# A graph layer's edge scatter on one core: twelve more quads take the grouped way

## The chip, the cores and the metric

One core of a Trainium2 chip. The metric is device time in microseconds, the median of several runs. TensorE is called PE here, VectorE DVE, ScalarE ACT, GpSimd POOL and SyncE SP. SP's queue only issues DMAs, in the order of the program, and a DMA whose wait isn't fulfilled holds up those behind it.

## The reference

A graph layer on 6250 nodes of 128 features and 200,000 edges. `dst` is sorted, so the gather from `x[idx_j]` reads nearly neighbouring rows; `src`, the target of the sum, is random.

```
idx_i, idx_j = src, dst                       # 200000 each
h    = relu(layernorm(x))                     # 6250 x 128
x1   = h @ W_in
W_ij = (softplus(f_ij @ W_f1 + b_f1) - ln 2) @ W_f2 + b_f2     # f_ij: 200000 x 20
x_ij = x1[idx_j] * (W_ij * f_ij_cutoff)
out  = segment_sum(x_ij, idx_i, 6250)
return x + (softplus(out @ W_o1 + b_o1) - ln 2) @ W_o2 + b_o2
```

## The kernel before

The edges are cut into chunks of 128 and quads of four chunks, 391 quads. One item of the main loop brings in one quad; the stages of a quad lie in successive items (`s1_`, `s2_`, `s3_`), and each item emits its instructions in fixed points: `L` (loads), `D0`, `D1`, `PE0`, `A0`, `A1`, `AX`, `DM`, `DR`, `PE1`, `PE2`, `A2`, `D2`, `S` (scatters). The table `AT` gives each step of the side work an offset in items and a point; `put` and `at` enter it there. What stands in one point of one item runs in the order in which it was entered. Nothing is reordered later.

Every quad has the same product: PE makes `z` (L374), ACT its softplus `a` (L379, L384), PE gathers `xg` by one-hots (L559) and multiplies `W` (L556, L567), ACT scales `xg` into `xc` (L572), DVE multiplies both (L582). Then there are three ways to the sum over `src`:

- Plain quads (the first of the ungrouped, `s3_pe`, `s3_copy`): a 128 x 128 equality matrix `eq` and matmuls `pp` (L594) add up edges of the same node in a chunk, and POOL scatters each chunk's sums `s` with its indices `ji` into one of four accumulators in HBM by an adding indirect DMA (L644, `acc<-s,ji`).
- Listed quads (every other ungrouped quad, `LB` to `LE`): the products `s` (six buffers) are scattered directly (L644, `acc<-s,lji`), four scatters for a quad. Edges whose node occurs twice in a chunk go to separate list rows (`l_eq`, `l_count` (L437), and twelve windows of 16 quads), which are summed at the end of a window (`l_load` L513, `l_sum` L531) and scattered once more.
- Grouped quads (`mpq`, in which `mpi` is the quad's number): no scatter for each chunk. DVE splits the product `pt` into three bf16 parts (L746), makes a permutation one-hot `pm` (L732) from a ranking for eight quads (`rank_*`, L655 to L725), PE permutes (`permute`, tile `pq`, L758), ACT copies (`perm_out`, tile `sg`, L766), SP regroups into `mst` (`regroup`, L773). Edges that overflow their group are summed for two grouped quads together (`over_*`: `po` L781, `mo`, `orow` L804, `oeq` L812, `osum` L818 to L820) and scattered once (`acc<-os,oji`).

Eight grouped quads form a round. A round is summed in four unit rounds: `unit_oh` makes a one-hot `so` (L845) for each quad, nine buffers, `unit_pe` multiplies 96 matmuls `un` (L860) into all four PSUM banks of tag `B`, and `unit_evac` adds these into the SBUF accumulator `accT` (L871). `unit_slots` places the four unit rounds over the time of the next round, in items that bring in a grouped quad whose third predecessor is not grouped. In such an item `permute` of the quad four items back moves to the item ahead.

Near the end, accumulator 0 gets no more scatters after the one numbered `RET`; `r0_load` (L1171, tile `r0t`) then fetches it, three items after the one with that scatter at the earliest, and PE transposes it (`rtp`, L1178). When all scatters have landed, a tail of 13 tiles adds up accumulators 1 to 3 and `accT` and multiplies by the output weights (from L1513).

Before, quads 8, 10, 12, ... 388 are grouped (191), 188 are listed and 12 plain.

Of the kernel before, what the change touches and what calls it, by code (L numbers as in the profile page):

```python
# [8 lines left out]
BF16 = mybir.dt.bfloat16  # L9
I32 = mybir.dt.int32  # L10
# [10 lines left out]
P = 128  # L21
# [5 lines left out]
OVC = 128  # L27
SLOTS = GRP * BCAP + OVC
MP0 = 8
MPGAPS = (2,)  # L30
MPEND = 1
RND = 8
RKQ = 8
ULAG = 7
# [41 lines left out]
def tile_gnn(ctx: ExitStack, tc: tile.TileContext, x, fB, cT, srcT, srcr, srci, dstr, win_, wf1, wf2, bias, bo1c, wo1,  # L76
# [25 lines left out]
    mpq = sorted_quads(NQ)  # L102
    mpi = {q: n for n, q in enumerate(mpq)}
    rounds = unit_rounds(mpq)
    uslots = unit_slots(rounds)
    units = {i for us in uslots for i in us}
# [31 lines left out]
    wk = edge.enter_context(tc.tile_pool(name="wk", bufs=2))  # L138
# [669 lines left out]
        mp[q]["row"] = t  # L808

    def over_eq(q):  # L810
        eq = wk.tile([P, P], BF16, tag="oeq", name="oeq", bufs=1)
        nc.vector.tensor_scalar(eq, mp[q].pop("row")[:, :P], mp[q]["so"], None, op0=ALU.is_equal)  # L812
        mp[q]["eq"] = eq

# [104 lines left out]
    with tc.manual_schedule():  # L919
# [126 lines left out]
        def at(i, point, fn, *a):  # L1046
            hooks.setdefault((i, point), []).append((fn, a))

        def put(name, base, fn, *a, busy=()):
            d, point = AT[name]  # L1050
            i = max(clear(base + d, busy) if busy else base + d, 0)
            at(i, point, fn, *a)
            return i
# [66 lines left out]
        busy = units | {prep_start(g) + k for g in range(1, NG) for k in range(5)}  # L1120
# [85 lines left out]
        if spread:  # L1206
            k = clear(mid + 9, busy, 2)
# [3 lines left out]
            k = clear(NQ - 1, busy, 2)  # L1211
# [25 lines left out]
        for r in range(-(-len(mpq) // RKQ)):  # L1237
# [5 lines left out]
            k = put("rk_count", i, rank_count, r, busy=units)  # L1243
            k = max(k + 1, i + AT["rk_own"][0])
            at(k, AT["rk_own"][1], rank_own, r)
            k = clear(max(k, i + AT["rk_over"][0]), units)
            at(k, AT["rk_over"][1], rank_over, r)
            k = max(k + 1, i + AT["rk_slot"][0])
# [5 lines left out]
        for w in range(NW):  # L1254
            for g in range(wsize[w] // 4):
# [9 lines left out]
                k = put("l_dup", i, l_dup, w, g)  # L1265
# [12 lines left out]
            k = clear(i + AT["l_sum"][0], units)  # L1278
# [4 lines left out]
            k = put("l_int", k, over_int, ("L", w))  # L1283
# [4 lines left out]
        for q in mpq:  # L1288
            put("pm", q, perm_oh, q)
            put("rem1", q, part_rem, q, 1)  # L1290
            put("rem2", q, part_rem, q, 2)
            put("ext", q, part_ext, q)
            if q + 4 in units:
                for s in range(4):
                    at(q + 3, "PE2", permute, q, s)
                for s in range(4):
                    at(q + 3, "PE2", perm_out, q, s)
                for h in range(2):
                    at(q + 4, "L", regroup, q, h)
            else:  # L1300
                for s in range(4):
                    put(f"p{s}", q, permute, q, s)
                    put(f"o{s}", q, perm_out, q, s)
                for h in range(2):
                    put(f"rg{h}", q, regroup, q, h)
            if mpi[q] % 2 or q == mpq[-1]:
                k = mpq[mpi[q] + 1] if mpi[q] + 1 < len(mpq) else q + 2
                put("over_pe", k, over_pe, q)
                put("over_out", k, over_out, q)
                put("over_idx", q, over_idx, q)  # L1310
                put("over_dg", q, over_dg, q)
                k = put("over_row", q, over_row, q, busy=units)
                put("over_eq", k, over_eq, q)
                k = put("over_sum", q, over_sum, q, busy=units)
                put("over_copy", k, over_copy, q)
                put("over_ji", k, over_ji, q)
                k = put("over_int", k, over_int, q)
                at(k, "S", over_scatter, q)
        last = mpq[-1]
        for r, us in enumerate(uslots):  # L1320
            for s, k in enumerate(us):
                for h in range(3):
                    d, point = AT[f"so{h}"]
                    at(max(k + d, us[s - 1] if s else uslots[r - 1][3] if r else 0), point, unit_oh, r, s, h)
                put("unit", k, unit_pe, r, s)
                put("evac", k, unit_evac, r, s)

# [100 lines left out]
    with tc.For_i(0, redo, 1):  # L1428
# [8 lines left out]
        with tc.For_i(0, trips, 1) as ci:  # L1437
# [12 lines left out]
                cm, engines=[SP], min_val=0, max_val=EP // P - 1,  # L1450
                skip_runtime_bounds_check_because="a column of the table")
            nc.sync.dma_start(xcol, dropd[:, bass.ds(cr, 1)])
            sb = wk.tile([P, P], I32, bufs=1, tag="oeq", name="fsb")
            nc.sync.dma_start(sb, srcr.rearrange("s e -> (s e)")[bass.ds(ci * P, P)].unsqueeze(0).to_broadcast([P, P]))
            ft = wk.tile([P, P], BF16, tag="oh", name="fft")
            nc.vector.memset(ft[96:P, :], 1.0)
# [32 lines left out]
            eq = wk.tile([P, P], F32, tag="eq", name="feq", bufs=3)  # L1489
# [3 lines left out]
            s = wk.tile([P, P], F32, bufs=1, tag="dg", name="fs")  # L1493
# [118 lines left out]
def sorted_quads(nq):  # L1612
    qs, q = [], MP0
    while q < nq - MPEND:
        qs.append(q)
        q += MPGAPS[(len(qs) - 1) % len(MPGAPS)]
    return qs
# [10 lines left out]
def unit_slots(rounds):  # L1628
    end = rounds[-1][-1]
    grouped = {q for qs in rounds for q in qs}  # L1630
    out, used = [], set()
    for r, qs in enumerate(rounds):
        a = qs[-1] + ULAG
        last = r == len(rounds) - 1
        step = 2 if last else (rounds[r + 1][-1] - qs[-1]) / 4
        us = []
        for s in range(4):
            i = a + int(s * step)
            while i in used or (not last and i <= end and not UCLASSES[UCLASS](i, grouped)):
                i += 1  # L1640
            used.add(i)
            us.append(i)
        out.append(us)
    return out
# [10 lines left out]
def clear(i, busy, n=1):  # L1655
    while any(i + k in busy for k in range(n)):
        i += 1
    return i
# [11 lines left out]
def prep_start(g):  # L1670
    busy = unit_its(sorted_quads(4 * PREP_GAP * (g + 8)))
    return clear(7 + PREP_GAP * (g - 1), busy, 2) - 1
# [100 lines left out]
```

## Time and profile before

| | |
|---|---|
| median of 3 runs | 1912.47 us (1911.3 to 1914.54) |
| the profiled execution | 1918.46 us, span 1916.7 us |
| mean granted clock of PE | 0.96 |
| instructions | 55067 |
| scatters on POOL | 907 (751 listed, 48 plain, 108 of sums) |
| items 0 to 390 end (last softplus) | at 1821 us |
| output tail | from 1867 us |

How to read the lines below. A group's row names line, engine, operation, tiles, shapes and count, then busy time in us and the mean length of one in ns, then the engine's idle time ahead of it with what ended that time. A stretch's row gives start and end, length, and for each engine that has work busy time and number of instructions, then PE's granted clock, the share of the DMA engines' time and GB/s; without a filter the engines are PE, PE's weight load (PEld), DVE, ACT, POOL. A wait's row has who waited for what, us in total, how often, and the longest. "issue" is time for which the profile shows no cause.

### The profile page before, as it was taken

Reading aid. Unit: us, or ns where it says so; the run is one execution under the profiler, and the core shown is the slowest. Engines: PE = TensorE matmul, PEld = TensorE weight load, DVE = VectorE, ACT = ScalarE, POOL = GpSimd, SP = SyncE. Lnnn points to the kernel's source line nnn. Section 1 sums busy time; section 2 is a strip of 40 time slices with the busy share of each in tenths; the row PEclk is TensorE's granted clock in tenths of the full one; section 3 lists DMA queues with packets and bytes.
Section 4 is the critical chain, followed back from the end, with each engine's and each line's share of the span. In section 5 each row is a group of like instructions: output and inputs, shape, how many; then the busy total and the mean of one; then the engine's idle time right before and its main releaser. Section 6 shows DMA issues by size and latency. Waiting matters only on the chain. (4 is left out here: it accounts for less than half of the span.)

```text
span 1916.7 us, 55067 instructions
## 1 busy us (share of the span) xinstructions
PE 1676.3 (87%) x19124; PEld 1142.4 (60%) x19124; DVE 1600.0 (83%) x4692; ACT 1449.6 (76%) x4045; POOL 1509.3 (79%) x960
## 2 busy tenths in 40 slices
PE   4678898989998989989989989999999999978976
PEld 3555566656666666665656656666666566655644
DVE  5768897988898899899889888898897897976657
ACT  4668777867887888887878878887887888866615
POOL 5577768778888888888888888888888888887755
PEclk8789999999999999999999999999999999998988
DMA  8888888878888888888888888888888888868757
GB/s 294 229 197 198 191 186 173 175 153 160 172 180 168 162 177 172 162 188 162 164 175 180 168 171 178 174 179 174 173 183 155 172 183 170 169 121 185 130 116 267
DMA packets 366238, 339.58 MB, mean 177 GB/s; under 512 B 86685, under 2 KB 329292, under 8 KB 365956
## 3 DMA queue, kind: packets, MB, share of 16 engines
q1 hardware_dynamic: 233189, 269.78, 49.5%
q0 software_dynamic: 132208, 66.05, 33.0%
q8 instruction: 151, 2.47, 0.5%
q14 instruction: 132, 1.07, 0.2%
q10 hardware_dynamic: 558, 0.20, 0.0%
HBM read 151.16 MB, written 108.80 MB: 136 GB/s over the span
## 5 line engine op out<-in xcount | busy, mean ns | idle before, releaser
L644 POOL DMA_INDIRECT acc<-s,lji x751 | 1210.0, 1611 | 269.4 <-issue 177.0
L572 ACT ACTIVATE xc<-xg,cb 128x128 f32<-128x128 f32 x1564 | 447.5, 374 | 179.7 <-PE z L374 92.5
L567 PEld LDWEIGHTS W<-w,a 128*128 128x128 f32 x3128 | 430.0, 199 | 64.2 <-issue 50.9
L860 PE MATMUL un<-so,mst 32*128 32x392 bf16 x9168 | 425.1, 329 | 18.1 <-ACT sg L766 7.9
L567 PE MATMUL W<-w,a 128*128 128x128 f32 x3128 | 430.7, 282 | 0.8 <-issue 0.5
L766 ACT CAST sg<-pq 128x388 bf16<-128x388 f32 x764 | 342.1, 497 | 75.0 <-DMA mst<-sg 48.5
L758 PE MATMUL pq<-pt,pm 128*128 128x388 bf16 x1528 | 328.5, 337 | 30.5 <-ACT os L825 9.6
L860 PEld LDWEIGHTS <-mst 32*128 32x128 bf16 x9168 | 251.5, 94 | 166.8 <-issue 37.6
L384 ACT ACTIVATE a<-a,con 128x512 f32<-128x512 f32 x391 | 282.8, 723 | 11.6
L746 DVE TENSOR_TENSOR pt<-pt 128x512 f32<-128x512 f32 x382 | 259.6, 680 | 0.0
L871 DVE TENSOR_TENSOR accT<-un,accT 128x392 f32<-128x392 f32 x368 | 182.1, 556 | 80.0 <-PE z L374 26.6
L379 ACT ACTIVATE a<-z 128x512 f32<-128x512 f32 x391 | 243.7, 623 | 6.3 <-PE z L374 6.3
L758 PEld LDWEIGHTS <-pm 128*128 128x128 bf16 x1528 | 143.6, 98 | 145.4 <-issue 56.9
L845 DVE TENSOR_SCALAR so<-iot,mst 128x392 bf16<-128x392 f16 x764 | 215.6, 333 | 4.3 <-PE un L860 2.9
L374 PE MATMUL z<-ft,ws 123*128 123x512 bf16 x391 | 154.8, 397 | 63.9 <-DVE s L582 13.2
L582 DVE TENSOR_TENSOR s<-W,xc 128x512 f32<-128x512 f32 x188 | 128.8, 685 | 93.8 <-ACT xc L572 56.5
L644 POOL DMA_INDIRECT acc<-os,oji x108 | 173.6, 1607 | 40.9 <-issue 18.3
L732 DVE TENSOR_SCALAR pm<-iotp,pos 128x384 bf16<-128x384 f16 x764 | 201.3, 323 | 0.0
L582 DVE TENSOR_TENSOR pt<-W,xc 128x512 f32<-128x512 f32 x191 | 130.4, 683 | 49.2 <-ACT xc L572 23.9
L559 PE MATMUL xg<-wn,oh 63*128 63x128 bf16 x1564 | 158.0, 222 | 12.1 <-DVE oh L391 7.3
L556 PE MATMUL W<-b2rep,onesb 64*128 64x512 bf16 x391 | 155.1, 397 | 0.0
L781 PE MATMUL po<-pt,pm 128*128 128x387 bf16 x764 | 153.1, 343 | 1.3 <-DVE pt L746 1.1
(214 smaller groups left out, 1840.9 us busy)
## 6 DMA issues: line engine op xcount, KB each, us to landing
mst<-sg SPq DMA_DIRECT2D x764, 97.0 KB
sb<-src SPq DMA_DIRECT2D x100, 256.0 KB
rb<-reld SPq DMA_DIRECT2D x194, 128.0 KB
fsd<-f SPq DMA_DIRECT2D x49, 480.0 KB
ft<-fsd SPq DMA_DIRECT2D x96, 240.0 KB
fb<-in_fB_dram SPq DMA_DIRECT2D x49, 320.0 KB
ft<-fsd SPq DMA_DIRECT2D x96, 160.0 KB
acc<-s,lji POOLq DMA_INDIRECT x751
```

The lines of the kernel that those rows point to most:

```text
L379: nc.scalar.activation(a, st[q]["z"], AF.Exp)
L384: nc.scalar.activation(a, a, AF.Ln, bias=half, scale=0.5)
L567: nc.tensor.matmul(W[:, c, :], st[q]["a"][:, c * P:(c + 1) * P], w2, start=False, stop=(c == 3))
L572: nc.scalar.mul(xc[:, c, :], st[q]["xg"][:, c, :], late["c", q // CQ][:, 4 * (q % CQ) + c:4 * (q % CQ) + c + 1])
L582: nc.vector.tensor_tensor(m[:, :, :P], st[q]["W"], st[q]["xc"], op=ALU.mult)
L644: nc.gpsimd.indirect_dma_start(out=accs[k][:rows, :], out_offset=bass.IndirectOffsetOnAxis(ap=ji, axis=0), in_=s, in_offset=None, compute_ ...
L732: nc.vector.tensor_scalar(pm[:, c], iotp, rk[r]["pos"][:, 4 * j + c:4 * j + c + 1], None, op0=ALU.is_equal)
L746: nc.vector.tensor_tensor(pt[:, :, k * P:(k + 1) * P], a, high(a), op=ALU.subtract)
L758: nc.tensor.matmul(t[:, :MW], mp[q]["pm"][:, c, s * P:(s + 1) * P], high(mp[q]["pt"][:, c:c + 1, :MW])[:, 0], start=(c == 2 * h), stop=(c ...
L766: nc.scalar.copy(mp[q]["sg", h][:, s], mp[q].pop(("q", k))[:, :MW])
L845: nc.vector.tensor_scalar(so, iotw[:, :GN], w[:, 3 * P // 2:3 * P // 2 + 1], None, op0=ALU.is_equal)
L860: nc.tensor.matmul(ts[g][:, :GN], mp[q]["ms", s // 2][v, s % 2, k * P:(k + 1) * P], mp[q]["oh"][v], start=(q == qs[0] and k == 0), stop=(q ...
```

## The change

`sorted_quads` now steps 2, 2, 2, 2, 1, 2, 2, 2, so that 15 items hold eight grouped quads where 16 did, and in every eight there is one pair in adjacent items. 203 quads are grouped, 172 listed (eleven windows) and 16 plain. There are 26 rounds, the last of three quads, where there were 24, the last of seven. Of a quad whose successor is grouped too, the second half of the copies and the regroup move to points `PE1` and `PE2` four items on. `oeq` gets a second buffer, the overflow sum is kept at least one item behind the row it needs, and a one-hot that would come earlier than the unit round ahead of it is written at the end of that round's item.

```diff
-MPGAPS = (2,)
-MPEND = 1
+MPGAPS = (2,2,2,2,1,2,2,2)
+MPEND = 2
...
-        eq = wk.tile([P, P], BF16, tag="oeq", name="oeq", bufs=1)
+        eq = wk.tile([P, P], BF16, tag="oeq", name="oeq", bufs=2)
...
                 for s in range(4):
                     put(f"p{s}", q, permute, q, s)
-                    put(f"o{s}", q, perm_out, q, s)
+                    if q + 1 in mpi and s > 1:
+                        at(q + 4, "PE1", perm_out, q, s)
+                    else:
+                        put(f"o{s}", q, perm_out, q, s)
                 for h in range(2):
-                    put(f"rg{h}", q, regroup, q, h)
+                    if q + 1 in mpi and h:
+                        at(q + 4, "PE2", regroup, q, h)
+                    else:
+                        put(f"rg{h}", q, regroup, q, h)
...
-                k = mpq[mpi[q] + 1] if mpi[q] + 1 < len(mpq) else q + 2
+                k = mpq[mpi[q] + 1] if mpi[q] + 1 < len(mpq) else q + 3
...
-                k = put("over_sum", q, over_sum, q, busy=units)
+                k = put("over_sum", max(q, k + 1 - AT["over_sum"][0]), over_sum, q, busy=units)
...
-                    at(max(k + d, us[s - 1] if s else uslots[r - 1][3] if r else 0), point, unit_oh, r, s, h)
+                    b = us[s - 1] if s else uslots[r - 1][3] if r else 0
+                    at(max(k + d, b), "D2" if k + d <= b else point, unit_oh, r, s, h)
```

The unit rounds stood four items apart (90 of 95 distances). Now they follow at distances of 2, 5, 4 and 4 (29 of 103 are 2). On DVE, in the middle of the program, the add into `accT` (four instructions) that empties the banks of one unit round, and the ten rows behind it, before:

```order
L871 TENSOR_TENSOR accT<-un,accT 128x392 x4
L582 TENSOR_TENSOR pt<-W,xc 128x4x128
L324 TENSOR_REDUCE fmax<-fb 128x1
L732 TENSOR_SCALAR pm<-iotp,pos 128x384 x4
L525 TENSOR_SCALAR leq<-orow,idl 128x128
L444 TENSOR_SCALAR ldup<-lcnt,con 128x16
L391 TENSOR_SCALAR oh<-rb,con 128x512
L746 TENSOR_TENSOR pt<-pt 128x4x128
L582 TENSOR_TENSOR s<-W,xc 128x4x128
L746 TENSOR_TENSOR pt<-pt 128x4x128
L845 TENSOR_SCALAR so<-iot,mst 128x392 x3
```

and now, at a place where two unit rounds stand two items apart:

```order
L871 TENSOR_TENSOR accT<-un,accT 128x392 x4
L582 TENSOR_TENSOR pt<-W,xc 128x4x128
L845 TENSOR_SCALAR so<-iot,mst 128x392 x3
L732 TENSOR_SCALAR pm<-iotp,pos 128x384 x4
L444 TENSOR_SCALAR ldup<-lcnt,con 128x16
L746 TENSOR_TENSOR pt<-pt 128x4x128
L582 TENSOR_TENSOR s<-W,xc 128x4x128
L746 TENSOR_TENSOR pt<-pt 128x4x128
L391 TENSOR_SCALAR oh<-rb,con 128x512
L830 SCALAR_TENSOR_TENSOR ojd<-os,con,ojd 128x1
L871 TENSOR_TENSOR accT<-un,accT 128x392 x4
```

Before, the first one-hots `so` of the next unit round come ten rows after the add and the next add into `accT` stands another 14 rows on; now five of them stand above these rows, ahead of the first add, the last three right behind it, and the next add follows ten rows after the first.

On POOL, in the middle of the program, scatters of listed products (`s,lji`) and of overflow sums (`os,oji`; the numbers tell the four accumulators apart), before:

```order
L644 DMA acc_77<-os,oji 6400x128
L644 DMA acc_78<-s,lji 7296x128
L644 DMA acc_75<-s,lji 7296x128
L644 DMA acc_76<-s,lji 7296x128
L644 DMA acc_77<-s,lji 7296x128
L644 DMA acc_78<-s,lji 7296x128
L644 DMA acc_75<-s,lji 7296x128
L644 DMA acc_76<-s,lji 7296x128
L644 DMA acc_77<-s,lji 7296x128
L644 DMA acc_78<-os,oji 6400x128
L644 DMA acc_75<-s,lji 7296x128
```

and now:

```order
L644 DMA acc_77<-s,lji 7168x128
L644 DMA acc_78<-os,oji 6400x128
L644 DMA acc_75<-os,oji 6400x128
L644 DMA acc_76<-s,lji 7168x128
L644 DMA acc_77<-s,lji 7168x128
L644 DMA acc_78<-s,lji 7168x128
L644 DMA acc_75<-s,lji 7168x128
L644 DMA acc_76<-os,oji 6400x128
L644 DMA acc_77<-s,lji 7168x128
L644 DMA acc_78<-s,lji 7168x128
L644 DMA acc_75<-s,lji 7168x128
```

Between two sums there stood eight listed scatters; now two sums stand together, then four listed scatters, then the next sum. In all POOL issues 687 listed, 64 plain and 113 other scatters, 864 for 907.

More of the change, by code (lines that the diff above doesn't have):

```diff
@@ L1452, in tile_gnn @@
             nc.sync.dma_start(xcol, dropd[:, bass.ds(cr, 1)])
-            sb = wk.tile([P, P], I32, bufs=1, tag="oeq", name="fsb")
+            sb = wk.tile([P, P], I32, bufs=2, tag="oeq", name="fsb")
             nc.sync.dma_start(sb, srcr.rearrange("s e -> (s e)")[bass.ds(ci * P, P)].unsqueeze(0).to_broadcast([P, P]))
```

## The prediction, made before the run

> **What bounds the kernel now.** I read the engine shares first, then the stretches of the main loop, then who waits for whom inside it, then the SP queue near the end. The two busiest resources are TensorE and the scatters on POOL:
>
> ```profile
> PE 1676.3 (87%) x19124; PEld 1142.4 (60%) x19124; DVE 1600.0 (83%) x4692; ACT 1449.6 (76%) x4045; POOL 1509.3 (79%) x960
> ```
>
> The stretches (time, then busy time of each engine) show a steady loop:
>
> ```profile
> 200.00:400.00 200.00, 180.57 (x2087) 122.54 (x2077) 173.41 (x527) 157.87 (x448) 151.27 (x96) 0.98 0.83 176
> 400.00:600.00 200.00, 181.33 (x2115) 123.17 (x2115) 173.10 (x535) 156.46 (x443) 165.92 (x103) 0.96 0.81 165
> 1200.00:1400.00 200.00, 186.54 (x2289) 126.11 (x2288) 172.94 (x493) 166.13 (x464) 166.64 (x106) 1.00 0.87 175
> 1400.00:1600.00 200.00, 184.52 (x2178) 124.15 (x2176) 175.56 (x515) 163.62 (x456) 168.25 (x104) 0.99 0.85 172
> ```
>
> PE is busy 90 to 93% at nearly its full clock. POOL does about 104 scatters in 200 us, one in 1.92 us. Its own waits between 200 and 1700 us:
>
> ```profile
> POOL acc L644 <- issue: 176.9, 572, 2.2
> POOL acc L644 <- DMA acc<-s,lji: 33.5, 70, 2.6
> ```
>
> 572 gaps of 0.31 us that nothing explains are the cost between two scatters, so POOL never rests either. Which of the two sets the pace? A scatter reads an `s` buffer (six of them, four scatters each, so 24 can be pending). The instructions on `s` from the start to 400, 1000, 1700 and 1850 us (DVE, ACT, POOL):
>
> ```profile
> 0.00:400.00 400.00, 23.07 (x42) 8.22 (x24) 239.38 (x148) 0.92 0.86 203
> 0.00:1000.00 1000.00, 67.60 (x107) 8.22 (x24) 674.88 (x418) 0.95 0.84 183
> 0.00:1700.00 1700.00, 122.39 (x188) 8.22 (x24) 1189.66 (x736) 0.97 0.85 179
> 0.00:1850.00 1850.00, 131.30 (x200) 8.22 (x24) 1291.38 (x800) 0.96 0.84 176
> ```
>
> 12 of the DVE instructions and 48 of the scatters belong to the quads that are neither listed nor grouped (the group `acc<-s,ji`, x48, below). So at 400 us 30 listed quads were written, 120 scatters, and 100 issued: 20 pending of 24. At 1000 us 95 and 370: 10 pending. At 1700 us 176 and 688: 16 pending. POOL runs behind all the way, but only before about 450 us is its backlog near the number of buffers. Who feels it? The longest waits of PE, and two of DVE, from 200 to 1700 us:
>
> ```profile
> PE hps L268 <- DVE accT L871: 12.2, 7, 3.5
> PE z L374 <- issue: 10.4, 27, 1.5
> PE z L374 <- DVE s L582: 10.1, 15, 0.9
> ```
>
> ```profile
> DVE s L582 <- issue: 21.0, 23, 3.2
> DVE s L582 <- DMA acc<-s,lji: 8.4, 4, 3.1
> ```
>
> No long wait of PE names a scatter, and DVE's wait for a free `s` is at most 29 us of 1500. From 450 us on PE sets the pace and POOL only just keeps up. One place is an exception. SP's load of accumulator 0 (L1171) waits for POOL's backlog, everything behind it on SP's queue waits too, and PE starves:
>
> ```profile
> SPq L1171 <- DMA acc<-os,oji: 16.3, 1, 16.3
> PE rtp L1178 <- DMA r0t<-acc: 11.6, 1, 11.6
> ```
>
> ```profile
> 1714.00:1731.00 17.00, 4.95 (x31) 3.90 (x30) 5.79 (x17) 4.05 (x13) 13.12 (x10) 0.63 0.56 95
> ```
>
> **The change part by part.** The two orders differ by these counts: PE gains 576 `un`, 96 `pq`, 48 `po` matmuls; DVE 24 `pt`, 48 `pm`, 48 `so`, 32 `accT`; ACT 48 `sg`; POOL loses 64 scatters of `s,lji` and gains 16 of `s,ji` and 5 of `os,oji`, 43 fewer; SP issues 48 more `mst`, 6 fewer `sb`, 4 fewer `lm`. The rows that price them:
>
> ```profile
> L860 PE MATMUL un<-so,mst 32*128 32x392 bf16 x9168 | 425.1, 329 | 18.1 <-ACT sg L766 7.9 <-issue 3.9 <-DVE so L845 1.5
> L758 PE MATMUL pq<-pt,pm 128*128 128x388 bf16 x1528 | 328.5, 337 | 30.5 <-ACT os L825 9.6 <-issue 4.2 <-ACT s L602 3.1
> L781 PE MATMUL po<-pt,pm 128*128 128x387 bf16 x764 | 153.1, 343 | 1.3 <-DVE pt L746 1.1 <-DVE accT L871 0.2
> L594 PE MATMUL pp<-m,eq 128*128 128x129 f32 x96 | 18.1, 353 | 8.9 <-DVE m L582 4.8 <-DVE jd L614 4.1
> L818 PE MATMUL osum<-mo,oeq 128*128 128x132 bf16 x96 | 21.1, 220 | 10.0 <-DVE accT L871 4.0 <-issue 3.9 <-DVE oeq L812 0.4
> L437 PE MATMUL lcnt<-wgtb,eql 128*128 128x1 bf16 x752 | 26.1, 163 | 14.3 <-DVE eql L427 7.1 <-ACT sg L766 5.8 <-DVE accT L871 0.7
> ...
> L746 DVE TENSOR_TENSOR pt<-pt 128x512 f32<-128x512 f32 x382 | 259.6, 680 | 0.0
> L845 DVE TENSOR_SCALAR so<-iot,mst 128x392 bf16<-128x392 f16 x764 | 215.6, 333 | 4.3 <-PE un L860 2.9 <-issue 0.8 <-DMA mst<-sg 0.6
> L732 DVE TENSOR_SCALAR pm<-iotp,pos 128x384 bf16<-128x384 f16 x764 | 201.3, 323 | 0.0
> L871 DVE TENSOR_TENSOR accT<-un,accT 128x392 f32<-128x392 f32 x368 | 182.1, 556 | 80.0 <-PE z L374 26.6 <-PE un L860 18.6 <-PE xg L559 16.0
> L766 ACT CAST sg<-pq 128x388 bf16<-128x388 f32 x764 | 342.1, 497 | 75.0 <-DMA mst<-sg 48.5 <-issue 11.7 <-PE pq L758 10.6
> ...
> L644 POOL DMA_INDIRECT acc<-s,lji x751 | 1210.0, 1611 | 269.4 <-issue 177.0 <-DMA acc<-s,lji 43.2 <-DVE pt L746 6.9
> L644 POOL DMA_INDIRECT acc<-s,ji x48 | 80.4, 1675 | 48.0 <-DMA acc<-s,ji 24.8 <-issue 11.1 <-DMA acc<-zero 6.1
> ```
>
> PE, busy time over count times the new instructions: `un` 576 x 425.1/9168 = 26.7 us, `pq` 96 x 328.5/1528 = 20.6, `po` 48 x 153.1/764 = 9.6. Four more quads take the plain way with its own combining matmuls (12 did before): 4 x 18.1/12 = 6.0. Six more overflow sums of three matmuls each: 18 x 21.1/96 = 4.0. The list counts give back 64 x 26.1/752 = 2.2. What else changes (two more ranking rounds and six overflow rows, one list window fewer) I put at about +2 from these neighbours. Sum 66.7. Ends of one group lie over starts of the next: eight `pq` in a row last 1.53 us and not the 1.72 that eight times 0.215 gives,
>
> ```profile
> 806.16 1.53 PE L758 MATMUL pq<-pt,pm 128*128 128x388 bf16 x8
> ```
>
> so I take a tenth off: **+60 us of PE**. This lies on the path, because PE is at 92% through the loop and its idle tenth comes from hand-overs to ACT and DVE which the new quads bring along too. Bounds: 30 if half of it fills holes, 72 if holes grow in proportion (66.7/0.92).
>
> DVE: 24 x 0.680 + 48 x 215.6/764 + 48 x 201.3/764 + 32 x 182.1/368 = 16.3 + 13.5 + 12.6 + 15.8 = 58 us, against 16 listed writes that turn into other writes of the same size. ACT: 48 x 342.1/764 = 21.5 us. Over a longer loop both stay at the shares of now, 87 and 82%, so they lie beside PE.
>
> POOL: 43 scatters fewer, 43 x (1.61 + 0.31) = 83 us less. Where PE sets the pace this buys nothing directly. It empties the backlog, which pays at two places. From 200 to 600 us PE's holes are 38.1 us of 400, from 1200 to 1600 us 28.9; the difference bounds the gain at 0 to 9: **-6**, since DVE's waits for `s` lie mostly there. At the load of accumulator 0, three items after the scatter it needs is scheduled, POOL will no longer be 16 scatters late. The 11.6 us of PE's wait, and one to two more for 4.95 us of work done at a clock of 0.63, go: **-13**, between 0 and -14. Late next there is the second load, which now waits for nothing longer than its neighbours.
>
> Closer unit rounds: 25 more pairs of them stand two items apart instead of four. DVE must write eight one-hots and drain four banks between them. The nearest rows are the last rounds of now, two apart with nothing between them, where PE pauses before the next round:
>
> ```profile
> 1857.19 0.32 PE L860 MATMUL un<-so,mst 32*128 32x392 bf16 x1 [1.08 <-DVE accT L871]
> ```
>
> In the body two items' own matmuls fill that, so I am nearer zero than 25 x 1.1: **+5**, between 0 and 27.
>
> The tail: the last round has three quads for seven, 36 matmuls for 84 in each of four unit rounds, but one more full round stands there. 336 `un` follow the last item's product for 432; the difference is already in the 576 and lies earlier. The last list's sum waits for its scatters there as now. I take 0, between -8 and +4. The second buffer of `oeq`, the later overflow sum, the 48 more `mst` stores (4.6 MB) and the moved copies and regroups I cost at nothing: the DMA engines are at 81 to 87% in the stretches above, and the fewer scatters give back about what the stores take; without that cover `un` would wait for `mst`.
>
> Sum: +60 - 6 - 13 + 5 = **+46**. The profiled execution took 1918.46 us (span 1916.7), 6 over the median of 1912.47; I add the sum to the median: **1958 us**.
>
> **The rivals.** *POOL is the pace.* For it: POOL has no free time, and DVE's waits name scatters. Against it: no PE wait does, and the backlog shrank from 20 to 10 between 400 and 1000 us with the scatter rate unchanged. If true, 43 scatters give 1912 - 83 = 1830 at most, and PE, with 1736 us of work, stops it near 1870. It decides if PE's holes fall below 6% of the loop. The Trainium skill ("Perfetto Trace Analysis", Identifying the Most-Contended Engine) speaks for this rival: it holds TensorE's matmul busy share for a poor measure and would have its headroom judged by the weight-load share. By that, 60%, PE would have room for the new matmuls and the sum would be about -83 instead of +46. The rows above differ from the rule here: in this loop PE's holes name DVE and ACT, and `pq` in a row run at their own length. Chance 0.08.
>
> *The holes swallow it.* If two thirds or more of the 60 us fit into PE's idle 8%, what remains is paid by the stall that goes: 1905 to 1925. Against it: DVE, at 87%, gets 58 us too, so the hand-overs do not get quicker. 0.12.
>
> *The close rounds pile up.* At 1.1 us or more for each of 25, and ACT behind in the adjacent quads' eight copies, +75 to +100: 1990 to 2010. 0.12.
>
> **How the numbers follow.** My own case has 0.68 and spans 1928 (30 of PE's work hidden: 30 - 6 - 13 + 5 = +16) to 1992 (72 of it, no early gain, no stall removed, +8 at the rounds: +80). The range over all cases, leaving out the first rival and half of each other, is 1918 to 1992. About 0.2% (4 us) is what a measurement of this kernel can tell from no change. Faster: 0.08 of the first rival and 0.06 of the second, 0.14. Same: 0.03 of the second. Slower: the rest, 0.83.
>
> **What would show it.** Right: PE busy near 1736 us with the loop still at 91 to 93%; POOL's waits no longer "issue" but for DVE's `s` products; no wait of SP at L1171 over 5 us and no hole of PE near it; scatters at 864. Wrong: PE at 95% or more and a span under 1905 (POOL was the pace), or `un` waiting for `accT` or `so` over 15 us in the loop (close rounds), or the hole at the accumulator load still there.

## The result and the profile after

| | before | after |
|---|---|---|
| median | 1911.88 us (4 runs, 1901.74 to 1914.54) | 2092.88 us (4 runs, 2087.19 to 2102.98) |
| ratio to before | | 1.0944, 95% interval 1.0894 to 1.0993 |
| the profiled execution, its span | 1918.46, 1916.7 us | 2087.19, 2085.4 us |
| granted clock | 0.960 | 0.947 |

181 us slower, where +46 was forecast. One execution of the run ret, at a granted clock of 0.83, is left out of its time below. The engines' row of the page of after:

```profile
PE 1772.9 (85%) x19842; PEld 1197.2 (57%) x19842; DVE 1659.3 (80%) x4858; ACT 1485.7 (71%) x4140; POOL 1435.1 (69%) x917
```

PE has 97 us more of busy time and 72 more of idle time, and no engine's share rose: the loop didn't run into a limit, it came apart into waits. Three groups of after, with the idle time of their engine ahead of them:

```profile
L644 POOL DMA_INDIRECT acc<-s,lji x687 | 1105.3, 1609 | 369.1 <-issue 159.5
L860 PE MATMUL un<-so,mst 32*128 32x392 bf16 x9744 | 481.1, 336 | 60.1 <-ACT sg L766 37.8
L766 ACT CAST sg<-pq 128x388 bf16<-128x388 f32 x812 | 364.0, 495 | 152.5 <-DMA mst<-sg 85.8
```

POOL now rests (369 us idle ahead of listed scatters for 269), as foreseen. What was not: ACT's copies into `sg` wait 86 us for the regroup store of an older `sg` (48.5 before), and `un` waits 38 us for such copies (7.9 before). ACT's wait, in total, how often, and the longest:

```profile
ACT sg L766 <- DMA mst<-sg: 85.8, 32, 8.7
```

The timeline shows one at an adjacent pair; a row gives start, length, what ran, and in brackets the idle time ahead and its cause. ACT, then PE, then SP's queue:

```profile
1041.91 0.85 ACT L766 CAST sg<-pq 128x388 bf16<-128x388 f32 x2
1043.66 0.90 ACT L766 CAST sg<-pq 128x388 bf16<-128x388 f32 x2
1045.11 0.87 ACT L766 CAST sg<-pq 128x388 bf16<-128x388 f32 x2
1054.72 0.87 ACT L766 CAST sg<-pq 128x388 bf16<-128x388 f32 x2 [8.74 <-DMA mst<-sg]
```

```profile
1047.63 0.34 PE L860 MATMUL un<-so,mst 32*128 32x392 bf16 x2
1055.25 7.33 PE L860 MATMUL un<-so,mst 32*128 32x392 bf16 x94 [7.29 <-ACT sg L766]
```

```profile
1050.17 1.15 SPq L773 DMA_DIRECT2D mst<-sg  x2
1051.99 4.72 SPq L773 DMA_DIRECT2D mst<-sg  x6
```

Two quads in adjacent items fill four `sg` tiles, and there are three buffers. The fourth tile's copies wait until the stores of the first have landed. The first tile is written by 1042.8 us, but its stores are issued only from 1050.17 us on: in between SP issues twelve other DMAs, which stand ahead of them on its queue. So of ACT's wait of 8.7 us, 4.2 lie before the store is issued and 4.5 behind. The unit round needs all four PSUM banks of tag `B`, one of which the waiting copy has not yet read out, so PE stands still for 7.3 us. And it comes back slow, as the granted clock (the last but two of each row) shows:

```profile
1044.00:1048.00 4.00, 3.96 (x30) 2.41 (x29) 4.00 (x14) 1.88 (x5) 3.46 (x2) 1.00 1.07 261
1048.00:1055.00 7.00, 0.00 (x0) 0.00 (x0) 0.49 (x1) 0.28 (x1) 1.84 (x1) 0.72 0.92 209
1055.00:1063.00 8.00, 7.75 (x100) 4.25 (x100) 2.72 (x9) 4.45 (x13) 4.06 (x3) 0.60 0.36 61
```

The 94 `un` behind the hole last 7.33 us; a whole round of before lasts 4.2:

```profile
1046.72 4.19 PE L860 MATMUL un<-so,mst 32*128 32x392 bf16 x96
```

So a hole of PE is paid twice, here with 7.3 and 3 us. The Trainium skill ("Perfetto Trace Analysis", Optimization Strategy) says that the same gap repeating on the engine that should be saturated can mean that there aren't enough buffers for the next tile; the trace agrees: ACT has 32 such waits, and PE 13 waits of `un` behind them.

### The profile page after: what moved, and what is told of

The parts are those of the page before. It is cut to its first block, busy times and chain, and to the rows that moved or that the text cites. A ratio compares the mean times of both kernels' runs of the same rounds, so it can differ in the third digit from the quotient of the medians.

```text
span 2085.4 us, 56776 instructions
## 1 busy us (share of the span) xinstructions
PE 1772.9 (85%) x19842; PEld 1197.2 (57%) x19842; DVE 1659.3 (80%) x4858; ACT 1485.7 (71%) x4140; POOL 1435.1 (69%) x917
## 5 line engine op out<-in xcount | busy, mean ns | idle before, releaser
L644 POOL DMA_INDIRECT acc<-s,lji x687 | 1105.3, 1609 | 369.1 <-issue 159.5
L860 PE MATMUL un<-so,mst 32*128 32x392 bf16 x9744 | 481.1, 336 | 60.1 <-ACT sg L766 37.8
L766 ACT CAST sg<-pq 128x388 bf16<-128x388 f32 x812 | 364.0, 495 | 152.5 <-DMA mst<-sg 85.8
L860 PEld LDWEIGHTS <-mst 32*128 32x128 bf16 x9744 | 284.9, 95 | 229.6 <-issue 91.3
L758 PE MATMUL pq<-pt,pm 128*128 128x388 bf16 x1624 | 360.8, 341 | 39.1 <-ACT os L825 7.6
L746 DVE TENSOR_TENSOR pt<-pt 128x512 f32<-128x512 f32 x406 | 276.6, 681 | 0.0
L871 DVE TENSOR_TENSOR accT<-un,accT 128x392 f32<-128x392 f32 x400 | 198.2, 557 | 91.8 <-PE un L860 40.0
L582 DVE TENSOR_TENSOR s<-W,xc 128x512 f32<-128x512 f32 x172 | 118.3, 688 | 147.2 <-ACT xc L572 110.6
L845 DVE TENSOR_SCALAR so<-iot,mst 128x392 bf16<-128x392 f16 x812 | 229.0, 335 | 6.7 <-PE un L860 5.3
L732 DVE TENSOR_SCALAR pm<-iotp,pos 128x384 bf16<-128x384 f16 x812 | 215.1, 325 | 0.0
```

The source lines that it names most:

```text
L582: nc.vector.tensor_tensor(m[:, :, :P], st[q]["W"], st[q]["xc"], op=ALU.mult)
L644: nc.gpsimd.indirect_dma_start(out=accs[k][:rows, :], out_offset=bass.IndirectOffsetOnAxis(ap=ji, axis=0), in_=s, in_offset=None, compute_ ...
L732: nc.vector.tensor_scalar(pm[:, c], iotp, rk[r]["pos"][:, 4 * j + c:4 * j + c + 1], None, op0=ALU.is_equal)
L746: nc.vector.tensor_tensor(pt[:, :, k * P:(k + 1) * P], a, high(a), op=ALU.subtract)
L758: nc.tensor.matmul(t[:, :MW], mp[q]["pm"][:, c, s * P:(s + 1) * P], high(mp[q]["pt"][:, c:c + 1, :MW])[:, 0], start=(c == 2 * h), stop=(c ...
L766: nc.scalar.copy(mp[q]["sg", h][:, s], mp[q].pop(("q", k))[:, :MW])
```

## The experiments

Each time is the median of at least four runs. The ratio, with its 95% interval, is that to the kernel before on the same chip (medians there 1912.5 to 1916.4).

### The ring of `sg` buffers

**sg4**: one more buffer; room for it comes from `s`. The ring of `sg` is shared with the equality matrices of the plain quads (tag `eq`), so their lines carry the same number.

```diff
-            mp[q]["sg", h] = wk.tile([P, 2, MW], BF16, tag="eq", name="sg", bufs=3)
+            mp[q]["sg", h] = wk.tile([P, 2, MW], BF16, tag="eq", name="sg", bufs=4)
...
-            m = sp_.tile([P, 4, 132], F32, tag="s", name="s", bufs=6)
+            m = sp_.tile([P, 4, 132], F32, tag="s", name="s", bufs=5)
...
```

> The changed kernel with four buffers for the half copies sg instead of three (and five for the products s, which pays for the space; after the change the scatters follow their products within about 3 us). Theory A, the ring: where two grouped quads are adjacent, four half copies are made within two items, the fourth waits for the store of the first (ACT waited 85.8 us for mst<-sg, 32 times), TensorE's unit round stands still behind it, and this is about 6 us in each of 26 places. Then this kernel takes 1960 to 1995 us. Theory B, plain overload: the work of two quads in the same two items is too much for ACT and DVE whatever the buffers; then 2060 us or more. Theory C, the closer unit rounds: also 2060 us or more.

Measured: 2015.99 us, 1.0536 [1.0484, 1.0588]: 77 us less than after. The time is above the 1960 to 1995 of theory A; 101 of the 181 us are left. But the wait of `sg` for its store fell from 85.8 to 0.5 us, and PE is at the busy time that the prediction's sum asked for (1736):

```profile
ACT sg L766 <- DMA mst<-sg: 0.5, 1, 0.5
```
```profile
PE 1735.2 (86%) x19842; PEld 1179.7 (59%) x19842; DVE 1662.5 (83%) x4858; ACT 1483.5 (74%) x4140; POOL 1441.0 (72%) x917
```

**sg5**: five for `sg`, four for `s`.

> The same with five buffers for sg and four for s. Theory A: no more than sg4, 1950 to 1990 us, and ACT's wait for mst<-sg under 30 us. Theories B and C: 2060 us or more, with the waits moved to other tiles.

Measured: 2012.93 us, 1.0528 [1.0486, 1.057]. A fifth buffer adds nothing: four are what a pair fills. This too is above its forecast, by the same rest.

**rg**: for quads whose regroup stands in the item of a unit round, it is issued at the end of the item ahead.

```diff
-                    at(q + 4, "L", regroup, q, h)
+                    at(q + 3, "D2", regroup, q, h)
```

> The changed kernel with three buffers, but the stores of a quad whose permutation precedes a unit round are issued at the end of that item, ahead of the next item's loads on SP's queue. Theory A with the queue as its second half: the store that frees the buffer no longer stands behind the loads, and the time falls to 1970 to 2040 us. If the ring alone matters and the queue does not, or if theory B or C holds: 2070 us or more.

Measured: 2084.89 us, 1.0898 [1.0851, 1.0945], and the wait for the store is what it was. Of a pair the edit moves the stores of the second quad alone. The store that frees the buffer is that of the first tile, which is issued at 1050.17 us in after and at 1050.37 here; whether an earlier place on SP's queue for that one would help was not tried.

```profile
ACT sg L766 <- DMA mst<-sg: 84.8, 30, 8.4
```

### The amount of work

**half**: one pair in every sixteen grouped quads, 197 grouped, 13 pairs.

```diff
-MPGAPS = (2,2,2,2,1,2,2,2)
+MPGAPS = (2,2,2,2,1,2,2,2,2,2,2,2,2,2,2,2)
```

> The changed kernel with one adjacent pair in sixteen grouped quads instead of eight: 197 grouped quads, 13 pairs. If the excess belongs to the pairs (theories A and B), it is halved: 1985 to 2015 us. If it comes from something that sets in at once, 2060 us or more.

Measured: 1999.91 us, 1.0481 [1.0428, 1.0533]: 88 of the 181 for half of the quads. But by the starts of `W` its first item comes at 44 us, where before it came at 18.5 and after at 29, so 25 of the 88 lie ahead of the loop. That led to **pad**, below.

**few**: the kernel before without the scatters of the first listed quad of each window.

```diff
             for c in range(nchunks(q)):
+                if k == 0:
+                    sc_n[0] += 1
+                    continue
                 scatter(st[q]["m"][:, c, :P], lst["ji", w][:, 4 * k + c:4 * k + c + 1], l_base(w) + P)
```

> The kernel before without the scatters of the first listed quad of each of the twelve list windows (48 of 907; that part of the sum is missing in the output). The term that the prediction gave to POOL: only the stall at the load of accumulator 0 and a few us of the early stretch follow from the backlog, so 1890 to 1912 us. The rival that POOL sets the pace: 48 x 1.9 = 91 us less, 1820 to 1835 us.

Measured: 1884.16 us, 0.986 [0.9821, 0.9899]. 48 scatters of 1.92 us are 92 us of POOL; 28 came through. POOL is not the pace, but its work counts with about a third.

**pe**: 14 more `un` matmuls in each unit round, 1344 in all.

```diff
+                if q == qs[0] and k == 0:
+                    for e in range(14):
...
+                        nc.tensor.matmul(ts[g][:, :GN], mp[q]["ms", s // 2][v, s % 2, :P], mp[q]["oh"][v],
+                                         start=False, stop=False)
```

> The kernel before with 14 more un matmuls in each of the 96 unit rounds (1344 repeats at 0.043 us, 58 us of TensorE and nothing for any other engine; the sums in the output are wrong by the repeats). The term of TensorE: what is added to its work lies on the path one for one, 1960 to 1980 us. The rival that the holes swallow it: under 1935 us.

Measured: 1922.94 us, 1.0056 [1.0033, 1.0078]. Ten us for an estimated 58 of PE: "PE sets the pace" fell. PE's busy time rose by 37 us only (1712.9 in the trace); the granted clock was higher too (0.969 for 0.960). By the starts of `W`, over the 55 unit rounds of items 130 to 346, a round's item became 0.77 us longer in the mean (5.85 to 6.62), and the three items behind it together 0.49 shorter. I read it so: during a round DVE and ACT catch up, and of what PE does longer there it waits less for afterwards.

**dve**: a one-hot of each grouped quad is written twice.

```diff
+        nc.vector.tensor_scalar(pm[:, 0], iotp, rk[r]["pos"][:, 4 * j:4 * j + 1], None, op0=ALU.is_equal)
```

> The kernel before with the first pm one-hot of each of the 191 grouped quads written twice: 191 x 0.32 = 62 us more of DVE, nothing else. PE alone gave +10 for 58. If DVE is the engine that sets the pace: +45 to +62, about 1965. If no engine alone does: +5 to +25, about 1925. If it lies beside other work altogether: under +4.

Measured: 1922.91 us, 1.0043 [1.0025, 1.0062], +9 for 62 us of DVE. Not DVE alone either.

**all3**: both of these edits, and the small copy behind `pt` twice (ACT), which by the count of ACT's instructions hit half of the quads and not three quarters. The added `un` do enter the sums; only the other two additions leave the output as it was.

> The kernel before with the twelve quads' extra work laid evenly over its loop, and nothing moved: 14 more un matmuls in each of the 96 unit rounds (about 58 us of PE, as in the run pe), the first pm one-hot of each of the 191 grouped quads written twice (191 x 0.32 = 62 us of DVE), the small ACT copy behind pt twice for three of four of them (143 x 0.22 = 32 us of ACT). The output stays as it was. Placement theory (the +100 us that stay in the changed kernel with four or five sg buffers come from two grouped quads in a row and rounds close together, not from the amount of work): 1930 to 1950, since spread work finds holes. Amount theory (PE, DVE and ACT at 87, 83 and 76% hand over to each other so often that work on all three of them counts nearly in full): 1975 to 2010.

Measured: 1960.68 us, 1.0231 [1.021, 1.0253], +46. Between the two theories: the three loads cost together more than twice the 19 that PE and DVE cost apart, and the work laid out evenly is still only a part of the changed kernel. ACT alone was not run; its 95 further copies of 0.22 us are 21 us, an estimate. And the 19 is too low for the loop. By the starts of `W`, one trace each, the stretch from item 0 to 360 is 18 us longer than before in pe, 18 in dve and 49 in all3, while that from 360 to 390 is 3, 12 and 5 us shorter. So in the loop each load counts with about a third of its work, and it isn't shown that the three together count for more.

```profile
PE 1727.5 (88%) x20468; PEld 1189.2 (61%) x20468; DVE 1646.5 (84%) x4883; ACT 1464.1 (75%) x4140; POOL 1513.8 (77%) x960
```

### The stall at the load of accumulator 0

**ret**: in the kernel before the last scatter into accumulator 0 comes 16 scatters earlier, and the load may come nine items after it instead of five.

```diff
-    RET = max(120, sum(scat) - 64)
+    RET = max(120, sum(scat) - 80)
-            i = clear(max(r0_at + 1, ret_at + 5), units)
+            i = clear(max(r0_at + 1, ret_at + 9), units)
```

> The kernel before, with accumulator 0 closed 16 scatters earlier while its load stays at the same items. The term of the stall: the load no longer waits for POOL's backlog and TensorE's hole of 11.6 us goes, 1895 to 1904 us. Otherwise the time stays at 1908 to 1918 us.

Measured: 1922.04 us (1907 to 1926), 1.001 [0.9972, 1.0048]: a gain of more than 5 us is ruled out. The load did not stay at its item; it is issued in item 368 for 372. SP's wait at it fell from 16.3 to 9.4 us and PE's from 11.6 to 5.0, so the stall is halved and not gone, and a later wait took its place:

```profile
SPq L513 <- DMA acc<-s,lji: 20.0, 3, 17.0
...
SPq L1171 <- DMA acc<-s,lji: 9.4, 1, 9.4
```

The time came back between the start of the last item's `W` and the tail (44 us before, 56 here). I take it that the scatters that are behind have to land in any case.

### The early load

**pad**: the changed kernel with 96 rows in the load of the narrow source ids; after has 94, before 100, half 97.

```diff
-    SR = -(-NS // 2)
+    SR = -(-NS // 32) * 16
```

> The changed kernel with one number changed: the load and the store of the narrow source ids take 96 rows in place of 94 (NS/2 rounded up to a multiple of 16; before it were 100). In the changed kernel that load of 376 KB crawls at some 50 GB/s until 17 us, in the run half (97 rows) at 27 GB/s until 25 us, before (100 rows) it is done by 11 us: I take it that the number of rows decides over how many of the 16 DMA engines it is spread. Expected by that: item 0 at 18 to 20 us in place of 29.5, and 8 to 12 us off the time, about 2082. If the late start has another cause (the order of the queues, the run): no difference.

Measured: 2079.32 us, 1.0862 [1.0844, 1.088], 14 less than after; the first item comes at 18.0 us for 29.0. From 11 to 15 us (half: 20 to 24), the stretches of before, after, half and pad show, last but one, the busy share of the 16 DMA engines, and then GB/s:

```profile
11.00:15.00 4.00, 0.00 (x0) 0.00 (x0) 3.29 (x13) 0.41 (x1) 1.22 (x2) 1.00 0.77 251
```
```profile
11.00:15.00 4.00, 0.00 (x0) 0.00 (x0) 0.91 (x3) 0.41 (x1) 0.00 (x0) 1.00 0.13 52
```
```profile
20.00:24.00 4.00, 0.00 (x0) 0.00 (x0) 0.00 (x0) 0.00 (x0) 0.00 (x0) 1.00 0.06 27
```
```profile
11.00:15.00 4.00, 0.00 (x0) 0.00 (x0) 3.29 (x13) 0.41 (x1) 1.14 (x1) 1.00 0.75 250
```

By the busy shares two engines of 16 (0.13) carry 94 rows, and one (0.06) carries 97, which is prime; with 100 and 96 the load is over by about 11 us, and other DMAs fill the stretch. The Trainium skill ("DMA: Bandwidth & Descriptors", Why a DMA increments its semaphore by 16 and not by 1) has the rule: a DMA runs on the largest number of engines up to 16 that divides the slowest dimension of both its sides, 10 for 100 rows and 16 for 96. The trace agrees for 94 and 97; how many engines 100 and 96 had can't be read here. A list of steps at the head of the kernel had changed the length of a load nine hundred lines away.

### Pairs and rounds

**apart**: in the changed kernel no unit round stands right behind a pair.

```diff
-UCLASSES = (lambda i, g: i in g and i - 3 not in g,
+UCLASSES = (lambda i, g: i in g and i - 3 not in g and not (i - 4 in g and i - 5 in g),
...
```

> The changed kernel with three buffers, but no unit round in the fourth item after the second quad of a pair; it moves two items on and stands two items ahead of the next, so there are about 24 more close rounds. Theory A in full: the jam needs the unit round, because it pulls all four permutations of the second quad into the item that holds the last two of the first. Then 1990 to 2040 us. If adjacency alone makes the jam: 2070 us or more. If close rounds cost over a microsecond each, 25 us are added to either.

Measured: 2052.09 us, 1.0735 [1.0698, 1.0773], 41 less, between its forecasts. `sg`'s wait for the store fell with it:

```profile
ACT sg L766 <- DMA mst<-sg: 38.6, 18, 4.2
```

Whether the gain was more than that, **sg4ap** tells: this edit with those of sg4 and pad.

> The changed kernel with three edits that were or are run alone: four sg buffers for three (2016 alone), no unit round right behind a pair of grouped quads (-40 alone, but at three sg buffers), 96 rows in the early load. Placement theory: the wait for sg gone, the pair and the round still share DVE and ACT, so taking them apart gives another 20 to 30 beside the 10 of the load: 1970 to 1985. Amount theory: the -40 was the wait for sg in another dress, and nothing but the 10 is left: about 2005, or worse by up to 10 for the 24 more rounds that stand close together.

Measured: 2020.6 us, 1.0563 [1.0539, 1.0587]. sg4 less the 11 to 14 of pad would be 2002 to 2005, so with enough buffers the edit costs 15 to 18: the 41 were the jam in another dress.

**pair3, pair4, close4** take the amount away: 191 grouped quads as before, with one pair in every eight. With the first gaps the rounds stay four items apart, with the second they stand at five, two and four, as in the changed kernel, though with 44 distances of five for its 24.

```diff
-MPGAPS = (2,2,2,2,1,2,2,2)
-MPEND = 2
+MPGAPS = (2,2,2,3,1,2,2,2)      # pair3; pair4 with the four sg and five s buffers
+MPGAPS = (2,3,2,2,1,2,2,2)      # close4, with these buffers too
+MPEND = 1
```

> The changed kernel's code with the gaps (2,2,2,3,1,2,2,2): 191 grouped quads as before, so none of the twelve quads' work, but in every eight one pair in adjacent items with a gap of three ahead of it. The unit rounds stand four items apart as before (90 of 95 distances), the mst buffers are as many, the early load has 100 rows. Ring theory (a pair has eight sg copies in two items and three buffers of two copies, so the last copies wait for the store of the first and un behind them): the wait of sg for the store 80 us or more, the body +60 to +85, about 1985. If the jam needs the further work or the close rounds: 1915 to 1935.

> As pair3 with four sg buffers (and five s for six). The placement of pairs alone, without the ring's jam, without work, without close rounds. If the rest of about 45 comes from two grouped quads in a row (DVE and ACT late behind twelve pq and eight po): 1945 to 1960. If from the close rounds or the work: 1912 to 1925.

> As pair4 with the gaps (2,3,2,2,1,2,2,2): 191 grouped quads with the pairs, and the unit rounds at distances five, two and four (44, 27, 24), nearly those of the changed kernel (24 of five, 29 of two, 47 of four). Against pair4 it prices the close rounds: my forecast had +5 (0 to 27) for 25 of them; the rival had 27 and more. I now expect +15 over pair4 if a close round costs 0.5 us or so, and +30 or more if the rest of 45 comes from there.

**old4** is the kernel before with four `sg` and five `s` buffers.

> The kernel before with four sg buffers and five s, nothing else. In it sg waits for its store for 48.5 us of 1916. If that wait costs PE: 1890 to 1905, and a version that beats both. If it lies beside other work: within 5 of before. If the fifth s buffer was worth something while POOL was behind (before 450 us): +3 to +10.

| | us | ratio to before |
|---|---|---|
| pair3 | 1948.01 | 1.0154 [1.0125, 1.0184] |
| pair4 | 1909.54 | 0.9948 [0.9923, 0.9973] |
| close4 | 1964.57 | 1.024 [1.0206, 1.0275] |
| old4 | 1918.98 | 1.0012 [0.9992, 1.0031] |

With pairs alone the ring costs 38 us (pair3 less pair4), without pairs nothing (old4). Pairs with enough buffers, and with the rest of the change's code, cost nothing; pair4 is even 7 us faster than before, a small gain but outside the noise, and the only version here that does the whole sum faster. The gaps that make the rounds uneven cost 55 (close4 less pair4). The longest waits of PE between 200 and 1700 us, pair4 and then close4:

```profile
PE z L374 <- DVE s L582: 29.9, 34, 5.6
PE un L860 <- ACT mo L786: 21.8, 21, 1.7
PE pq L758 <- DVE rank L699: 20.9, 18, 1.8
```
```profile
PE lcnt L437 <- DVE eql L427: 56.2, 20, 3.6
PE z L374 <- ACT a L379: 27.8, 28, 1.2
```

These 20 waits of up to 3.6 us come once in 16 items, in the third of the four items between two rounds that stand five apart. By the starts of `W` (items 226 to 354) that item lasts 7.44 us for 3.58 in pair4. PE and DVE there in close4:

```profile
1192.46 0.34 PE L437 MATMUL lcnt<-wgtb,eql 128*128 128x1 bf16 x8
1195.49 0.37 PE L437 MATMUL lcnt<-wgtb,eql 128*128 128x1 bf16 x8 [2.68 <-DVE eql L427]
1195.72 1.46 PE L758 MATMUL pq<-pt,pm 128*128 128x388 bf16 x4
```

```profile
1183.00:1189.00 6.00, 6.00 (x58) 4.15 (x51) 5.08 (x14) 3.69 (x11) 5.09 (x4) 1.00 0.62 88
1189.00:1192.00 3.00, 2.13 (x15) 1.26 (x14) 3.00 (x8) 2.97 (x10) 2.39 (x3) 1.00 0.64 128
1192.00:1196.00 4.00, 1.32 (x23) 1.05 (x22) 3.96 (x12) 1.70 (x8) 2.92 (x2) 0.64 0.97 197
1196.00:1199.00 3.00, 3.00 (x15) 1.91 (x14) 2.27 (x7) 2.97 (x9) 1.75 (x1) 0.50 0.59 106
```

The third busy time is DVE's: full from 1189 to 1196, while PE has run out of work. The short gap isn't where it costs. My reading is that a round gives PE 4.2 us of work in which DVE catches up, and that behind two rounds close together the next one comes too late. It isn't shown alone. In the same 16 items there is a second distance of five, between the rounds of items 234 and 239 for instance, and it has no such wait. The costly one also holds the second half of the pair, a ranking, and the list count `lcnt`, which the edit moved along: it stands in item 228 here, and in pair4 in 227, right behind the round of 226. In sg4, whose rounds stand around each pair as here, most list counts fall elsewhere, and PE waits for `eql` 5 times:

```profile
PE lcnt L437 <- DVE eql L427: 12.2, 5, 2.8
```

So the 55 us are the price of these gaps in this kernel, and how much of it the changed kernel pays stays open.

In and behind the hole the clock is 0.64 and 0.50, and the four `pq` last 1.46 us for 0.85 at full clock. The same 19124 matmuls have 1679.1 us of busy time in close4 and 1642.7 in pair4: 36 of the 57 us between the spans are PE running longer, 20 its idle time. The mean clocks, 0.948 and 0.962, account for some 24 of the 36 (1.5% of 1643); the other 12 stay open.

**even4** and **even3** were to confirm it in the changed kernel, with 96 rows and with four or three `sg` buffers, by letting rounds stand in any item:

```diff
-UCLASS = 0
+UCLASS = 3
```

> The changed kernel with four sg buffers (five s), 96 rows in the early load, and the rule that a unit round stands in a grouped item three behind an ungrouped one dropped: rounds at distances four, four, three, four in the loop (72 of four, 24 of three, 5 of two) in place of 47 of four, 24 of five and 29 of two. If the stretches of five items without a round are what costs (in the run close4 PE waits 3.6 us in one item of each of them): before + 46 for the work - 7 for the pairs = 1950 to 1960. If that cost belonged to the pattern of close4 alone: about 2000, as the run sg4 less the load.

> As even4, but with the changed kernel's three sg buffers and six s. If the ring costs what it costs with pairs alone (pair3 less pair4, 38): 1990 to 1998, so 85 of the changed kernel's 181 go by two edits that need no memory. If it costs 77 as in the changed kernel: about 2030.

Measured: 2128.15 us, 1.1116 [1.109, 1.1141], and 2140.27 us, 1.1166 [1.1137, 1.1196], both slower than after. So these runs confirm nothing. The rule that I dropped kept rounds out of the items in which a quad's overflow matmuls (`po`) stand. Now three rounds of four share an item with eight `po` and four `pq`, which use the same banks, and that item lasts 10.8 us, 8.7 of them PE; `un` waits for copies:

```profile
PE un L860 <- ACT sg L766: 92.3, 72, 1.8
```

PE's long items then stand next to three short ones (2.5 to 3.6 us). Evenness in items isn't evenness in work. Between these two the ring costs only 12 us, so its price hangs on what stands around it: 77, 38 or 12. What the changed kernel would do with even rounds free of `po` was not tried.

## Why the prediction was wrong

The direction held, the size did not: +181 for +46, outside the range. The step that failed first is the term that was put at nothing, the moved copies and their stores. By the prediction's own steps:

- **"I cost at nothing" (moved copies and regroups, 48 more `mst`): the largest miss, 77 us.** The cover that I named was the DMA engines' load. The resource was the number of `sg` buffers against the time until a store has landed. The row stood in the prediction: `sg`'s idle time of 48.5 us behind `mst<-sg`. I read it as ACT's slack and didn't count that a pair fills four tiles where there are three buffers. A fourth buffer takes 77 us away (sg4) and costs or gains nothing where there are no pairs (old4).
- **"+60 us of PE, on the path".** The work was sized right (1735 us of PE where the ring doesn't jam), but not its place: 58 us of PE alone cost 10. The premise that PE at 92% sets the pace is what was wrong here. The rival "the holes swallow it" was right for PE alone, and its counter-argument was as well: DVE and ACT get their share too, and the three loads together cost 46. That it equals the +46 of the forecast is chance; the forecast had 60 there.
- **"Closer unit rounds +5 (0 to 27)": 55 in close4**, a kernel without the further quads. I priced the pause between the two rounds that stand close; the trace has the loss in the long distance behind them, where PE waits for DVE's `eql`. In the changed kernel this wait comes 7 times, 16.7 us in all, so the size of the term there stays open. The sign that I had named for it did not come: `un` waits for `accT` 3.3 us in all. The rival "the close rounds pile up" had 75 to 100 for it and for ACT behind the pairs' copies; it was the nearest, and had 0.12.
- **"-13 for the stall": not settled.** The stall did go: in after SP's longest wait at the load is 3.3 us. ret, which halves it in the kernel before, loses at the end what it gains (1.001). But in sg4, sg5 and dve, where PE's hole is gone too, items 360 to 390 last 142.8, 142.8 and 143.5 us for 155.5 before, and what follows them is no longer than before by more than 1 us. So there the term is about as large as forecast. In after these items last 152.2 us, with two long waits of `un` for `sg` among them.
- **"-6 for POOL" stays open.** The run few shows that 48 scatters are worth 28 us in the kernel before. In the changed kernel POOL waits for products instead (the next row, over the whole span; 3.7 us before), and its gain wasn't taken apart from the terms above.

```profile
POOL acc L644 <- DVE s L582: 145.8, 57, 6.0
```

- **Not in the sum at all: the early load, 11 us by the trace, 14 by the medians.** I had noted fewer ungrouped quads and not what is sized by their number; the rule cited above would have told it from 94 and 100.
- The rival "POOL is the pace" fell. Of the rule that the prediction cites for it (the Trainium skill, "Perfetto Trace Analysis", Identifying the Most-Contended Engine) one half held: PE did have room. But with work for DVE and ACT beside it the cost was 46 us for 10, and the weight-load share, 61% in pe and in all3 alike, doesn't tell these two apart.

In the changed kernel itself two terms are measured, the ring with 77 us and the load with 11 to 14. Laid beside them, the work of all3 (46) and the pairs of pair4 (-7) make 127 to 130 of the 181. The 55 of close4 would make it 184 or so, but its wait is mostly absent there, and the ring's own price moves between 12 and 77. The runs that were to show that the terms add up in one kernel (even4, even3) failed for a reason of their own. So some 50 us stay open; that they belong to the uneven rounds is likely and not shown.

Of the signs that were named, these came: POOL's scatter instructions 43 fewer, POOL waiting for products, no long wait of SP at L1171. The loop at 91 to 93% did not: between 200 and 1600 us PE is at 86 to 90%.

## What to carry to other kernels

When a change puts two producers next to each other, count the buffers of every tile that they fill against the time until the last reader (a store too) lets go; a wait that costs nothing now (48.5 us before) can be the first to cost when the rhythm changes. In this loop, with four engines at 76 to 87%, no engine's added time counted one for one: it counted with about a third, for PE and DVE alone and for the three loads together (ACT alone was not tried). Don't call the busiest engine the pace before a run has added work to it alone. A long block of one engine may be where the others catch up, so look at what stands in the longest stretch without one. Look also at what is sized by a number that the change moves, the rows of a load above all.

## What the runs showed of the hardware

- PE's clock was halved around a hole of only 2.7 us. In close4 the hole begins at 1192.8 us; the granted clock is 1.00 up to 1193 us, 0.56 in the next one, 0.50 from 1194 to 1199 and 1.00 again from 1200. So it fell as the hole began, behind 2 us in which PE was busy 0.49 and 0.64 of the time, and stayed low for some 4 us after the hole. Behind the hole of 7.3 us in after it is 0.60 for 8 us. Of close4's loss of 57 us more lies in PE's longer busy time than in its holes.
- While a load of some 380 KB crawled with hardly another beside it, the DMA engines moved 27 GB/s with 97 rows and 52 with 94; it was over by 25 and 18 us, with 96 or 100 rows by 11.
